# A graph kernel's set-up stage: chunk bases by a product, node rows loaded ahead of the edge sources, scaling one group at a time, and checks and late weights moved into the first pass

## The chip, the cores and the metric

The kernel runs on one core of a Trainium2 chip. The metric is the device time of one execution in microseconds (us), as a median over runs. The engines are TensorE (PE; its weight loads are shown as PEld), VectorE (DVE), ScalarE (ACT), GpSimd (POOL) and SyncE (SP). Each engine works through its own queue of instructions; SP only issues DMA transfers here.

## The reference

There are 12,500 nodes with 256 features and 200,000 edges sorted by their destination. First a graph-convolution layer with a residual, then an attention layer with a residual. Cut to what matters:

```python
def gcn_conv(x, W, b, src, dst, n):          # src, dst with a self-loop per node added
    h = x @ W
    deg = segment_sum(ones, dst, n)
    dinv = where(deg > 0, rsqrt(deg), 0)
    return segment_sum(h[src] * (dinv[src] * dinv[dst])[:, None], dst, n) + b

h = maximum(layernorm(x), 0)
h = relu(gcn_conv(h @ W_pre + b_pre, W1, b1, ...))
h = relu(gcn_conv(h, W2, b2, ...))
x = x + (h @ W_post + b_post)
h = maximum(layernorm(x), 0); xt = (h @ weight).reshape(n, 4, 64)
# alpha: softmax over 4 heads, from xt[src], xt[dst] of the first n edges and attn_l, attn_r
x = x + mix of xt[dst[:n]] by alpha, broadcast to the 4 heads
```

## The kernel before, in words

The fast path has a set-up stage, two convolution passes over all edges, and a short attention stage at the end. If a check fails (`bad_row` above 0) a general path runs afterwards; it does not run on these inputs.

The edges are cut into 112 chunks (`NCH`) of 1792 (`CE`), a chunk into 14 tiles (`J`) of 128. In a pass (`convolve`) GpSimd gathers one tile's 128 source rows with one indirect DMA into `fgot` (L999, 64 buffers), VectorE makes one-hot matrices of a chunk's destinations (`fhot`), and TensorE adds the rows up by products (L1004). When a tile of 128 nodes is complete, the steps of `finish1` (first pass) or `finish2` (second) follow; `e()` is the last of `finish1`.

The set-up stage, which the change is about, makes what the first gather needs: `ftable1`, the 98 tiles of normalised and scaled node rows, in DRAM, and `src_t`, the source numbers turned so that they can index. It goes like this.

- SP loads `dst_r` and `src_r` (111 full rows of 1792 numbers and a last, shorter one), then x in 14 groups of 7 tiles (`load_x`, tile `fxt`, L585). There are 11 buffers (`XB`), so groups 11 to 13 are loaded once groups 0 to 2 have been written to the table.
- GpSimd issues 30 small DMAs that pick every tile's first destination (`a_raw`), and then fills constants: `sel`, `iota_r`, `iota_a`, `slide`, `zeros`.
- VectorE makes `dst_f` and `near_f` of `dst_r`; ScalarE makes `src_f` of `src_r` (L636). TensorE and VectorE multiply W_pre by W1 (`wp`, `wpt`, `wf`, L651 to L664).
- TensorE clears the counts with `zeros` (L671) and turns `near_f`, the destinations and the sources in 4 groups each (`turned`, L680), copied out by VectorE (`near_t`) and ScalarE (`to_t`, `src_t`, L685). Two PSUM buffers called `ft` alternate.
- Degrees are counted in 16 blocks, 4 for each of 4 parts. For a block `count_block` lets VectorE make one-hots (`hot_r`, L699) and TensorE add them up; `stats` makes the layernorm sums of one x group. After a part's last block `place` moves the counts to node order: `tiles_b` (ScalarE, L720), `hot_n` (VectorE, L722), `count` and `fdegs` (TensorE). `norms` makes the scales of a part's node tiles and then scales all its groups in one go (3, 3, 4 and 4 groups of 7 tiles, L773 to L785), each followed by its write to the table. It runs for a part one block after the next part has begun; for the last part at the end.
- Then VectorE runs the checks (L804 to L852), and the weights that are needed later are loaded by ScalarE's queue and worked on by VectorE (L869 to L886). The first gather follows.

The work is emitted under a manual schedule: each engine takes its instructions in the order in which the code gives them. So where a line stands decides what waits behind it.

Of the kernel before, what the change touches and what calls it, by code (L numbers as in the profile page):

```python
# [8 lines left out]
F32 = mybir.dt.float32  # L9
# [8 lines left out]
P = 128  # L18
# [395 lines left out]
def fast_path(  # L414
# [69 lines left out]
    nc.vector.memset(eps, EPS)  # L484

# [7 lines left out]
    row_i = const.tile([P, AC], I32, name="row_i")  # L493
    lane = const.tile([P, 1], F32, name="lane")
    nc.gpsimd.iota(lane, pattern=[[0, 1]], base=0, channel_multiplier=1,
                   allow_small_or_imprecise_dtypes=True)

    def load_w(w, name):
        t = const.tile([P, KC, w.shape[1]], F32, name=name)
        nc.scalar.dma_start(t, w.rearrange("(k p) n -> p k n", p=P))  # L500
        return t
# [5 lines left out]
    with tc.tile_pool(name="fprep", bufs=1) as prep:  # L507
# [34 lines left out]
        src_r = load_edges(src, 0, "fsrc_r")  # L542
# [8 lines left out]


        a_raw = prep.tile([I, NPT, L], I32, name="a_raw")
        nc.gpsimd.memset(a_raw, NOWHERE)
        for k in range(NPT):
            whole = min(E // CE - k * CP, CP)
            d = dst[k * CP * CE:(k * CP + whole // L * L) * CE].rearrange(
                "(q l j e) -> j q l e", l=L, j=J, e=P)
            a = a_raw[:, k, :].rearrange("(j q) l -> j q l", q=Q)
            for q in range(whole // L):  # L560
                nc.gpsimd.dma_start(a[:, q, :], d[:, q, :, 0])
            for l in range(whole % L):
                c = k * CP + whole // L * L + l
                nc.gpsimd.dma_start(
                    a[:, whole // L, l:l + 1],
                    dst[c * CE:(c + 1) * CE].rearrange("(j e) -> j e", e=P)[:, 0:1])
        if last < CE:
            j = -(-last // P)
            e = (NCH - 1) * CE
            a = a_raw[:, NPT - 1, L - 1:L].rearrange("(j q) l -> j q l", q=Q)[:, Q - 1]  # L570
            for n in range(j):
                nc.gpsimd.dma_start(a[n:n + 1], dst[None, e + n * P:e + n * P + 1])
# [19 lines left out]
        for g in range(XB):  # L592
            load_x(g)

# [3 lines left out]
        for r0, base, keep in ((0, 0, [-1, LB - 1]), (R, LB, [1, -LB])):  # L600
# [5 lines left out]
        iota_r = prep.tile([P, R, JB * CP], BF16, name="iota_r")  # L606
        nc.gpsimd.iota(iota_r, pattern=[[1, R], [0, JB * CP]], base=0, channel_multiplier=0,
                       allow_small_or_imprecise_dtypes=True)
# [57 lines left out]
        with tc.tile_pool(name="fpsum", bufs=2, space=PSUM) as psum, \  # L666
# [92 lines left out]
            def norms(k):  # L759
# [11 lines left out]
                for g in range(w0 // G, w1 // G):  # L771
# [14 lines left out]
                    if g + XB < NG:  # L786
                        load_x(g + XB)
# [3 lines left out]
            for s, (k, j0) in enumerate(blocks):  # L791
                count_block(k, j0)
                if s < NG:
                    stats(s)
# [493 lines left out]
```

## Time and profile before

| what | value |
|---|---|
| time of the kernel, median of 3 runs | 4307.19 us (4305.39 to 4313.39) |
| the profiled execution's own time | 4960.23 us |
| span in that profile, first to last instruction | 4958.2 us |
| POOL busy, gathers of L999 | 2984.3 us, 3126 of them, 955 ns each |
| PE busy | 2964.7 us |
| DVE busy | 1148.5 us |
| first gather of the first pass starts | 162.01 us |

Busy times and starts are of the one profiled execution, counted from the start of its span. That execution took 653 us longer than the median run. "Idle before" in a row of the profile names what ended the engine's idle time in front of an instruction; "issue" means that nothing the profile shows was waited for.

### The profile page before, as it was taken

The page shows a single profiled execution, that of the slowest core. Times are in us where ns is not written, and L with a number is a line of the kernel's source. Part 1 is how long each engine was busy: PE and PEld are TensorE (multiplying, and loading weights), DVE is VectorE, ACT ScalarE, POOL GpSimd, SP SyncE. Part 2 cuts the span into 40 slices and gives each one's busy share as a digit, 9 for nine tenths or more (in the row PEclk, how much of TensorE's full clock was granted, in tenths as well). Part 3 has the DMA queues.
Part 4 walks back from the last instruction along what each step waited for, and adds up shares of the span by engine and source line. Part 5 has one row for each costly group of instructions (what it writes and reads, how often), then busy time and mean ns, then how long its engine had stood idle before and what let it go on. Part 6 is the DMA issues. An engine that isn't in the chain of part 4 may idle for free.

```text
span 4958.2 us, 34772 instructions
## 1 busy us (share of the span) xinstructions
PE 2964.7 (60%) x10827; PEld 2202.3 (44%) x10827; DVE 1148.5 (23%) x2468; ACT 383.4 (8%) x1054; POOL 3115.8 (63%) x3297
## 2 busy tenths in 40 slices
PE   5345555564555556465626767666777677677853
PEld 4133444343343334344414555555555555555642
DVE  7211111121111212112202222222222222222227
ACT  3100000000000000000000000000000000000112
POOL 2566666666666666666466666666666666666533
PEclk7567777677777777777757777777777777777766
DMA  5433333333333333333333443444444443444335
GB/s 179 133 93 105 106 106 105 104 108 104 106 105 105 104 105 106 105 106 104 101 93 112 113 112 105 113 108 107 110 109 109 110 108 108 109 110 108 97 97 157
DMA packets 301046, 543.62 MB, mean 110 GB/s; under 512 B 84021, under 2 KB 199476, under 8 KB 300852
## 3 DMA queue, kind: packets, MB, share of 16 engines
q0 software_dynamic: 154480, 414.28, 31.3%
q1 hardware_dynamic: 114926, 111.19, 7.4%
q10 hardware_dynamic: 31446, 15.83, 1.1%
q8 instruction: 88, 1.44, 0.1%
q14 instruction: 106, 0.87, 0.1%
HBM read 488.01 MB, written 52.93 MB: 109 GB/s over the span
## 4 chain that ended last, share of the span: by engine, by line
another core or an unknown queue 36%; PE 32%; issue 19%; DVE 4%; ACT 3%; POOL 1%; DMA 1%; ACTq 0%; DVEq 0%; POOLq 0%; SPq 0%
PE facc L1004 18%; PE fpo L1092 3%; PE fpo L1039 2%; PE fpx L1128 2%; PE fpo L1093 2%; PE fpo L1040 1%; POOL fgot L999 1%; PE fturn L952 1%; ACT h L1113 1%; PE fpt L1014 1%; PE fpz L1080 1%; DVE fhot L939 1%; DVE fx L1097 1%; PE fpz L1082 1%
## 5 line engine op out<-in xcount | busy, mean ns | idle before, releaser
L999 POOL DMA_INDIRECT fgot<-ftable,fsrc_t x3126 | 2984.3, 955 | 1595.4 <-issue 822.5
L1004 PE MATMUL facc<-fgot,fhot 128*128 128x257 f32 (+1 forms) x6252 | 1901.8, 456 | 218.1 <-issue 157.2
L1004 PEld LDWEIGHTS facc<-fgot,fhot 128*128 128x128 f32 x6252 | 1392.8, 233 | 564.6 <-issue 297.0
L952 PE MATMUL fturn<-fident,fsums 128*128 128x128 f32 x448 | 117.3, 355 | 626.9 <-issue 484.8
L939 DVE TENSOR_TENSOR fhot<-iota_p,to_t 128x1792 f32<-128x1792 f32 x224 | 447.6, 2000 | 0.1
L952 PEld LDWEIGHTS fturn<-fident,fsums 128*128 128x128 f32 x448 | 75.9, 184 | 690.4 <-issue 529.0
L946 ACT ACTIVATE fsums<-facc 128x257 f32<-128x257 f32 (+1 forms) x224 | 86.2, 385 | 3586.5 <-remote 2411.7
L1097 DVE SCALAR_TENSOR_TENSOR fx<-fpo,fdinv,fxb 128x256 f32<-128x256 f32 x98 | 47.4, 484 | 1289.1 <-PE fpo L1093 837.2
L1039 PE MATMUL fpo<-wf,fin 128*128 128x256 f32 x392 | 142.4, 499 | 329.1 <-issue 242.9
L1128 PE MATMUL fpx<-fwg,ht 128*128 128x4 f32 (+1 forms) x392 | 99.1, 363 | 391.3 <-ACT ht L1120 359.5
L1033 DVE TENSOR_TENSOR fin<-buf,fpt 128x256 f32<-128x256 f32 x98 | 41.1, 420 | 1205.5 <-remote 916.9
L962 DVE TENSOR_TENSOR buf<-buf,fturn 128x256 f32 x224 | 94.5, 422 | 949.8 <-PE facc L1004 414.4
L1128 PEld LDWEIGHTS fpx<-fwg,ht 128*128 128x128 f32 x392 | 88.6, 300 | 427.4 <-ACT ht L1120 388.7
L1039 PEld LDWEIGHTS fpo<-wf,fin 128*128 128x128 f32 x392 | 93.8, 252 | 362.0 <-issue 330.3
L1092 PE MATMUL fpo<-fwo,fz 128*128 128x256 f32 x392 | 171.8, 584 | 80.7 <-ACT fz L1087 78.8
L1199 POOL DMA_INDIRECT fal<-table_l,fsrc_t x98 | 94.0, 959 | 140.4 <-ACT fxg L1192 84.6
L1080 PE MATMUL fpz<-fin,fwb 128*128 128x128 f32 x784 | 147.5, 317 | 10.3 <-issue 10.3
L1092 PEld LDWEIGHTS fpo<-fwo,fz 128*128 128x128 f32 x392 | 104.7, 291 | 102.2 <-ACT fz L1087 83.4
L1080 PEld LDWEIGHTS fpz<-fin,fwb 128*128 128x128 f32 x784 | 118.3, 215 | 26.6 <-issue 16.3
L1190 PE MATMUL fends<-rows,hot_t 128*128 128x260 f32 x196 | 71.2, 517 | 86.8 <-issue 48.4
L1014 PE MATMUL fpt<-fident,self 128*128 128x128 f32 x392 | 100.6, 343 | 22.4 <-issue 19.6
L1014 PE MATMUL fpt<-fident,h 128*128 128x128 f32 x196 | 42.7, 303 | 108.6 <-ACT h L1113 83.0
(176 smaller groups left out, 1754.9 us busy)
## 6 DMA issues: line engine op xcount, KB each, us to landing
fgot<-ftable,fsrc_t POOLq DMA_INDIRECT x3126
ftable<-fxt SPq DMA_DIRECT2D x14, 910.0 KB
self<-ftable SPq DMA_DIRECT2D x98, 130.0 KB
ftable<-fo ACTq DMA_DIRECT2D x98, 128.0 KB
self<-ftable SPq DMA_DIRECT2D x98, 128.0 KB
kept_x<-fx SPq DMA_DIRECT2D x98, 128.0 KB
fxr<-kept_x SPq DMA_DIRECT2D x14, 896.0 KB
fxb<-in_x_dram SPq DMA_DIRECT2D x97, 128.0 KB
```

The source lines that it names most:

```text
L939: nc.vector.tensor_tensor(h[:, :n, :], iota_p[:, None, :].to_broadcast([P, n, P]), to_t[:, c, :n, None].to_broadcast([P, n, P]), ALU.is_equal)
L952: nc.tensor.transpose(v["pt"][:, k, :], sb[:, k * P:(k + 1) * P], ident)
L962: nc.vector.tensor_add(b, b, v["pt"][:, :KC, :])
L999: nc.gpsimd.indirect_dma_start(out=got, out_offset=None, in_=table[:], in_offset=bass.IndirectOffsetOnAxis(ap=src_t[:, c, j:j + 1], axis=0))
L1004: nc.tensor.matmul(acc, hots[c][:, j, :], got[:, :width], start=(j == 0), stop=(j == nj[c] - 1))
L1014: nc.tensor.transpose(pt[:, k, :], s[:, k * P:(k + 1) * P], ident)
L1039: nc.tensor.matmul(po, v["f"][:, k, :], wf[:, k, :], start=(k == 0), stop=False)
L1080: nc.tensor.matmul(pz[:, m, :], wb[:, k, m * P:(m + 1) * P], v["f"][:, k, :], start=(k == 0), stop=False)
L1092: nc.tensor.matmul(po, v["z"][:, m, :], wo[:, m, :], start=(m == 0), stop=False)
L1093: nc.tensor.matmul(po, v["rm"], bor, start=False, stop=True)
L1097: nc.vector.scalar_tensor_tensor(x2, v["po"], dinv[:, w:w + 1], v["x"], op0=ALU.mult, op1=ALU.add)
L1128: nc.tensor.matmul(px[:, d0:], v["ht"][:, k, :], wg[:, k, d0:], start=(k == 0), stop=(k == KC - 1))
```

## The change

- The chunk tiles' first destinations no longer come by 30 small DMAs. Three VectorE operations and one TensorE product (`low_q`, `by_kl`, `pa`) make them from `low`; the product stands behind all three calls of `turned`. The four operations that make `a_bf` move from the first `place` to the front of the first block.
- `src_r` is loaded after x groups 0 and 1 instead of ahead of x. GpSimd's constants change their order: `zeros`, `slide` and `iota_r` first.
- `dst_f` is gone: `near_f` and `to_f` are made of `dst_r` directly.
- ScalarE instead of VectorE copies `wpt`, `wf`, `bb` and `near_t`. A ScalarE operation on `eps` (`warm`) is put at the very front.
- `stats` runs one block ahead. `norms` only puts its groups in a list; `scale` takes one group per block, and the rest of the list before the last `norms`, with VectorE's help. The copy of `dinv` into the rows moves to GpSimd. One reciprocal for `dinv2` at the end replaces four.
- Part of the checks becomes small GpSimd operations early in the set-up stage; the rest (`check_chunks`) and the loading of the late weights (`load_late`) are emitted in the first pass, behind the first finished node tile.

The diff, cut to its core:

```diff
+    warm = const.tile([P, 1], F32, name="warm")
+    nc.scalar.activation(warm, eps, AF.Sqrt)
...
-        src_r = load_edges(src, 0, "fsrc_r")
...
-        a_raw = prep.tile([I, NPT, L], I32, name="a_raw")
-        nc.gpsimd.memset(a_raw, NOWHERE)
-        for k in range(NPT):
-            whole = min(E // CE - k * CP, CP)
...
-                nc.gpsimd.dma_start(a[:, q, :], d[:, q, :, 0])
...
         for g in range(XB):
             load_x(g)
...
+            if g == 1:
+                src_r = load_edges(src, 0, "fsrc_r")
...
+        zeros = prep.tile([1, 512], BF16, name="zeros")
+        nc.gpsimd.memset(zeros, 0.0)
...
+        perm = prep.tile([NCH, Q, NPT, L], F32, name="perm")
+        nc.gpsimd.memset(perm, 0.0)
+        nc.gpsimd.affine_select(out=perm, in_=perm, compare_op=ALU.not_equal, fill=1.0, base=0,
+                                pattern=[[-L, Q], [-CP, NPT], [-1, L]], channel_multiplier=1)
...
-        dst_f = prep.tile([NCH, CE], F32, name="fdst_f")
-        nc.vector.tensor_copy(dst_f, dst_r)
...
-                                dst_f.rearrange("c (j e) -> c j e", e=P),
+                                dst_r.rearrange("c (j e) -> c j e", e=P),
...
+        by_q = prep.tile([NCH, Q], F32, name="by_q")
+        nc.vector.tensor_reduce(by_q, perm.rearrange("c q k l -> c q (k l)"), AX.X, ALU.add)
+        by_kl = prep.tile([NCH, NPT, L], F32, name="by_kl")
+        nc.vector.tensor_reduce(by_kl, perm.rearrange("c q k l -> c k l q"), AX.X, ALU.add)
+        low_q = prep.tile([NCH, J, Q], F32, name="low_q")
+        nc.vector.tensor_mul(low_q, low[:, :, None].to_broadcast([NCH, J, Q]),
+                             by_q[:, None, :].to_broadcast([NCH, J, Q]))
         base = prep.tile([NCH, 1], F32, name="base")
-        nc.vector.tensor_copy(base, dst_f[:, 0:1])
-        to_f = dst_f
-        nc.vector.tensor_scalar(to_f, dst_f, base, None, op0=ALU.subtract)
+        nc.vector.tensor_copy(base, dst_r[:, 0:1])
+        to_f = prep.tile([NCH, CE], F32, name="fto_f")
+        nc.vector.tensor_scalar(to_f, dst_r, base, None, op0=ALU.subtract)
         src_f = prep.tile([NCH, CE], F32, name="fsrc_f")
         nc.scalar.activation(src_f, src_r, AF.Copy)
...
+        nc.gpsimd.tensor_scalar(mean, mean, 0.0, None, op0=ALU.max)
+        mean_i = prep.tile([NCH, 1], I32, name="mean_i")
+        nc.gpsimd.tensor_copy(mean_i, mean)
+        nc.vector.tensor_scalar(mean_i, mean_i, ~(P - 1), None, op0=ALU.bitwise_and)
...
+        nc.gpsimd.tensor_sub(off, base, off)
...
-                nc.vector.tensor_copy(wpt[:, k, :], pt)
+                nc.scalar.activation(wpt[:, k, :], pt, AF.Copy)
...
-                nc.vector.tensor_copy(wf[:, i, :], pw)
+                nc.scalar.activation(wf[:, i, :], pw, AF.Copy)
...
-            nc.vector.tensor_copy(bb[:1, :], pw[:1, :])
+            nc.scalar.activation(bb[:1, :], pw[:1, :], AF.Copy)
...
-            turned(near, near_t, nc.vector.tensor_copy)
+            turned(near, near_t, by_act)
             turned(to_f, to_t.rearrange("p c j -> p j c"), by_act)
             turned(src_f, src_t.rearrange("p c j -> p j c"), by_act)
-            a_int = prep.tile([I, NPT, L], I32, name="a_int")
             a_bf = prep.tile([I, NPT, L], BF16, name="a_bf")
+            pa = psum.tile([I, NPT, L], F32, name="ft")
+            nc.tensor.matmul(pa, low_q.rearrange("c j q -> c (j q)"), by_kl, start=True, stop=True)
...
-                for g in range(w0 // G, w1 // G):
-                    t = xs[g]
-                    nc.vector.tensor_copy(t[:, :, D], dinv[:, g * G:(g + 1) * G])
-                    for i in range(G):
-                        w = g * G + i
-                        h = t[:, i, :D]
-                        if k == NPT - 1 and i % 2:
-                            nc.vector.tensor_scalar(h, h, sc[:, w:w + 1], nb[:, w:w + 1],
-                                                    op0=ALU.mult, op1=ALU.add)
-                            nc.vector.tensor_scalar(h, h, 0.0, None, op0=ALU.max)
-                        else:
-                            nc.scalar.activation(h, h, AF.Relu, bias=nb[:, w:w + 1],
-                                                 scale=sc[:, w:w + 1])
-                    nc.sync.dma_start(
-                        table1[g * G * P:(g + 1) * G * P, :].rearrange("(c p) d -> p c d", p=P), t)
-                    if g + XB < NG:
-                        load_x(g + XB)
-                nc.vector.reciprocal(dinv2[:, w0:w1], deg[:, w0:w1])
-
+                to_scale.extend(range(w0 // G, w1 // G))
+
+            to_scale = []
+
+            def scale(both):
+
+                g = to_scale.pop(0)
+                t = xs[g]
+                nc.gpsimd.tensor_copy(t[:, :, D], dinv[:, g * G:(g + 1) * G])
+                for i in range(G):
+                    w = g * G + i
+                    h = t[:, i, :D]
+                    if both and i % 2:
+                        nc.vector.tensor_scalar(h, h, sc[:, w:w + 1], nb[:, w:w + 1],
+                                                op0=ALU.mult, op1=ALU.add)
+                        nc.vector.tensor_scalar(h, h, 0.0, None, op0=ALU.max)
+                    else:
+                        nc.scalar.activation(h, h, AF.Relu, bias=nb[:, w:w + 1],
+                                             scale=sc[:, w:w + 1])
+                nc.sync.dma_start(
+                    table1[g * G * P:(g + 1) * G * P, :].rearrange("(c p) d -> p c d", p=P), t)
+                if g + XB < NG:
+                    load_x(g + XB)
+
+            stats(0)
+            for k in range(NPT):
+                nc.vector.tensor_scalar(a_bf[:, k, :], pa[:, k, :], 1.0 / LB, -float(a_of[k]),
+                                        op0=ALU.mult, op1=ALU.add)
             blocks = [(k, j0) for k in range(NPT) for j0 in range(0, J, JB)]
             for s, (k, j0) in enumerate(blocks):
                 count_block(k, j0)
-                if s < NG:
-                    stats(s)
+                if s + 1 < NG:
+                    stats(s + 1)
                 if j0 + JB >= J:
                     place(k)
                 if k and j0 == JB:
                     norms(k - 1)
+                if to_scale:
+                    scale(False)
+            while to_scale:
+                scale(True)
             norms(NPT - 1)
+            while to_scale:
+                scale(True)
+            nc.vector.reciprocal(dinv2, deg)
...
-        nc.vector.tensor_reduce(lo, to_f, AX.X, ALU.min)
...
+        nc.tensor.transpose(pk[:, 0, :NCH], off, ident[:NCH, :NCH])
+        nc.vector.tensor_copy(offs, pk[:, 0, :NCH])
...
+    def check_chunks(work, psum):
+
+        last = E - (NCH - 1) * CE
+        far = work.tile([P, 2, NCH], F32, name="far2", bufs=1)
+        nc.vector.tensor_reduce(far[:, 0, :], to_t, AX.X, ALU.min)
+        c, (n, r) = NCH - 1, divmod(last, P)
...
+    def load_late(work):
+
+        for t, w in ((wb, w2), (wo, w_post), (wg[:, :, :D], w_gat)):
+            nc.scalar.dma_start(t, w.rearrange("(k p) n -> p k n", p=P))
+        nc.scalar.dma_start(b2r, b2[None, :])
+        nc.scalar.dma_start(bor, b_post[None, :])
+
         for i, a in enumerate((attn_r, attn_l)):
-            ar = work.tile([P, D], F32, name="far")
+            ar = work.tile([P, D], F32, name="far", bufs=1)
             nc.scalar.dma_start(ar, a.rearrange("h c -> (h c)").partition_broadcast(P))
...
+            if w == 0:
+                load_late(work)
+                check_chunks(work, psum)
```

## The prediction

> **What bounds the kernel now.** I read the page first: its head and the costliest row.
>
> ```profile
> span 4958.2 us, 34772 instructions
> L999 POOL DMA_INDIRECT fgot<-ftable,fsrc_t x3126 | 2984.3, 955 | 1595.4 <-issue 822.5
> ```
>
> Each gather takes 0.955 us and the next starts 0.30 us later in the timeline, so 3126 of them need at least 3126 × 1.25 = 3908 us. In this profile they come every 1.43 us. The median run, 4307.19 us, is 653 us below the profiled 4960.23, and if I take away the set-up (162), the gap between the passes (44) and the end (280), it has 3821 us or 1.22 us for each gather. So GpSimd's issuing paces both passes, and whatever moves the first gather moves the end, one for one. I take differences from the profile's set-up and put them on the median, which assumes that the set-up stage itself is not stretched by profiling.
>
> Next, the set-up in windows of 2 us (columns: PE, PEld, DVE, ACT, POOL busy; clock; DMA share; GB/s).
>
> ```profile
> 12.00:14.00 2.00, 0.00 (x0) 0.00 (x0) 0.00 (x0) 0.00 (x0) 2.00 (x4) 1.00 0.22 76
> 18.00:20.00 2.00, 0.00 (x0) 0.00 (x0) 1.93 (x4) 0.00 (x0) 2.00 (x4) 1.00 0.21 79
> 34.00:36.00 2.00, 0.32 (x1) 0.12 (x2) 0.00 (x0) 0.00 (x0) 1.66 (x5) 0.50 1.01 331
> ```
>
> For 10 us only 0.21 of the 16 DMA engines, about three, are moving data: the loads of `dst_r` and `src_r`, one after the other. Then the timeline of the front:
>
> ```profile
> 17.37 1.09 DVE L621 CAST fdst_f<-fdst_r 112x1792 f32<-112x1792 int32 x1 [14.94 <-DMA fdst_r<-in_dst_dram]
> 29.28 1.28 ACT L636 ACT_TABLE_LOAD   x1 [29.28 <-DMA fsrc_r<-in_src_dram]
> 35.68 1.03 PE L671 MATMUL count<-zeros 1*32 1x512 bf16 x2 [8.27 <-POOL zeros L617]
> 40.25 2.02 DVE L699 TENSOR_TENSOR hot_r<-near_t,iota_r 128x3584 bf16<-128x3584 bf16 x1
> ```
>
> ScalarE stands still until `src_r` has landed at 29.3; TensorE waits for `zeros`, last in GpSimd's queue. From 40.25 VectorE is busy nearly without a hole until 119.2. The timeline of the stage's end:
>
> ```profile
> 117.47 1.73 DVE L722 TENSOR_TENSOR hot_n<-a_bf,iota_a 56x1526 bf16<-56x1526 bf16 x1
> 128.01 0.33 ACT L720 ACTIVATE tiles_b<-tiles 56x224 bf16<-56x224 f32 x1
> 134.22 0.19 DVE L763 TENSOR_SCALAR fdeg<-fdegs 128x28 f32<-128x28 f32 x1 [15.02 <-PE fdegs L747]
> 143.79 1.96 DVE L804 TENSOR_REDUCE flo<-fdst_f 112x1 f32<-112x1792 f32 x1
> 162.01 1.04 POOL L999 DMA_INDIRECT fgot<-ftable,fsrc_t  x1 [63.64 <-issue]
> ```
>
> `tiles_b` waits 8.8 us behind 28 scalings on ScalarE. From 143.8 the checks and the late weights run. SP's waits say when the table was complete:
>
> ```profile
> SPq L1023 <- DMA ftable<-fxt: 8.8, 1, 8.8
> ```
>
> SP stood at 144.1, so the table landed at 152.9; the gather came 9.1 us later, behind VectorE's work on the weights.
>
> **The change, part by part.** Front first. `src_r` now stands behind x groups 0 and 1 on SP's queue. A group is 0.92 MB; its sixteenth, 57 KB, takes 2.3 us on an engine at 76/3 = 25 GB/s. The Trainium skill, "DMA: Bandwidth & Descriptors", says why this costs the full amount: under "Why a DMA increments its semaphore by 16 and not by 1", a DMA gets the largest number of engines up to 16 that divides the outer size (111 rows: 3), and under "Queues, rings and completion order", descriptors of one ring are consumed in order. The measured 0.21 of 16 agrees. So `src_r` lands at 29.3 + 2 × 2.3 = 33.9. Were it not held up in the ring, it would stay at 29.3; I take the ring. The 30 small DMAs gone may give it up to 1 us back; I count nothing.
>
> ScalarE's queue still has `src_f` at its head, and now `wpt`, `wf`, `bb` and `near_t` are copied by ScalarE behind it, so TensorE waits too. Step by step: `src_f` 1.70 (no table load now, `warm` did it: 1.28 saved) to 35.6; two `wpt` copies at about 0.42 (`fsums`, 385 ns, is the nearest row) to 36.5; the W products took 22.46 to 27.41, 4.95, to 41.5; `bb` 0.4; zeros 1.03, to 43.0. `zeros` itself is no longer waited for, nor GpSimd: its constants are then 14 us of rows that show, starting at 2. Twelve groups are turned: four copied by ScalarE took 40.09 to 44.19, 4.10, so 12.3, to 55.3. Here a rule speaks for less. "ScalarE: Activation LUTs", under "What ACT_TABLE_LOAD costs", gives an immediate-operand ACTIVATE 186 ns + 0.833 ns per column, 559 ns for 448 columns; the trace's median for `to_t` is 948. By the rule the twelve groups would take 12.3 − 6 × 0.39 = 10.0, as every second copy is on the path. The trace decides. Then `pa` (two matmul records of 0.39, overlapping) 0.5 and `a_bf` 0.7: the first `hot_r` starts at 56.5 instead of 40.25. x, loaded early or not, has all landed by then, so its earlier start buys nothing.
>
> Costed at nothing in the front, because VectorE, GpSimd and the first weight loads have nothing to do with the wait for `src_r`: `dst_f` gone (1.09), the three operations that prepare `pa`, and the weight loads' issue behind `warm` (a table load of 1.28; the product of `wp` is wanted at 36 now). If `src_r` came at 20, the first two would be on the path with about a microsecond each way. The 14 or so small GpSimd operations of the moved checks have no near row; between 0.14 (the iota of `fmean`) and 1.08 (a select on `sel`) each, they take 2 to 15 us, begin when `base` is there at 21, and are wanted only at the stage's end. VectorE's one operation among them waits for GpSimd's constants, until 16, with nothing behind it before 56.
>
> The blocks, VectorE: 78.95 us before (40.25 to 119.2). Gone are `stats(0)`, which fits in the wait (2.77), a hole of 1.07, `a_int` and `a_bf` 0.5, ten `dinv` copies 0.73, three reciprocals 0.6: 5.7 less, 73.3. So the last `hot_n` ends at X = 129.8, 10.6 later than the 119.2 before. GpSimd's `dinv` copies (between a 0.13 memset and 0.3) may wait behind a `load_x` memset for a table write (8.7 us in the trace), but x groups 11 to 13 are wanted 20 us later.
>
> The tail, from X. ScalarE has groups 6 and 7 ahead of `tiles_b`: 14 × 0.49 = 6.9 us, begun 4.7 before X, so `tiles_b` starts at X + 2.3 (before: X + 8.8). With count 1.4 and `counted` 0.7 it is X + 5.0; group 8 (3.4) and four of group 9 (2.0) stand ahead of the last `froot`, which comes at X + 10.5 though `fdegs` is ready at X + 8.6 (before: X + 15.2). New wait, small: ScalarE's queue. Then 1.0 for the scales, 8.2 for four groups as before: X + 19.7. Their writes move at about 350 GB/s, 2.65 us each, follow that of group 9 at X + 15.2, and land at X + 26.6; the 0.79 MB of weights no longer share the DMA. VectorE's remaining small checks (some 5 us behind X + 19.7) end before that. Gather at X + 27.0 = 156.8, against 162.0: **5.2 us earlier**. The tail wins 15.8 (6.5 for `tiles_b`, 9 behind the table), the front and blocks give back 10.6.
>
> Moved into the first pass: four products and reductions 4 × 0.836 = 3.3, two reductions of 1568 columns (1.96 for 1792: 1.7 each), a dozen small ones at 0.15 to 0.28: about 9 us of VectorE, and a wait of up to 8 for seven DMAs on ScalarE's queue (issues 0.41 to 1.32 before). Queued behind it are `fhot` of the next chunk and the `buf` additions, so TensorE may stand up to 17 us. GpSimd waits for none: it has 64 buffers, 80 us. Cost 0 if so; at most 2, if a gather here and there takes 1.45 instead of 0.95 as at 999.7; I take 0.5. Without those buffers all 17 would count.
>
> Sum: 4307.2 − 5.2 + 0.5 = **4302.5 us**.
>
> **Rivals.** (A) The front is set back less: `src_r` lands near 29, or copies run by the rule, and the first `hot_r` starts by 53. Each us comes off one for one. Were `src_r` waited for only where it is turned, TensorE would reach `pa` near 40: gain 21, 4286. With 4.6 + 2.3 together: 12, 4295. For it: the 3 engines leave 13 idle. Against: ScalarE's 29.28 us of waiting in front of L636. (B) Slower: `src_r` loses more to x. Each further x group that gets onto its three engines ahead of it adds 2.3 to 2.6; with two the gain is gone, from six on it is slower by over 0.2%, all nine give + 22: 4324. For it: SP's x issues follow at once. Against: ring order. (C) The late work reaches GpSimd: only if VectorE is held for over 75 us; nothing shown is that long.
>
> **How the numbers follow.** 0.2%, 8.6 us, is about what a measurement of this kernel can tell from no change. The likeliest case (0.51) has `hot_r` uncertain by 2.5 and the tail by 3: 4297 to 4308, within 0.2%. A gets 0.42, since three separate steps can each turn out shorter, and B and C 0.07 together. The range reaches into A: 4286 to 4310.
>
> **What would show it.** In the changed profile: ScalarE idle to about 34 in front of `src_f`; first `hot_r` at 54 to 59, behind `a_bf`; x complete before it; last `tiles_b` about 2 us behind `hot_n`; first gather near 157, as the table lands; VectorE waiting in the first pass once, with GpSimd's gathers undisturbed. A first `hot_r` below 50, or a first gather below 152, would make me wrong on the fast side; `src_r` landing past 40 on the slow side.

## The result, and the profile after

| | before | after |
|---|---|---|
| time, median | 4303.65 us (7 runs) | 4292.27 us |
| ratio to before, 95% interval | | 0.9973 [0.9963, 0.9984] |
| first gather of the first pass | 162.17 us | 153.86 us |
| first `hot_r` | 40.55 us | 53.27 us |

The kernel became 11.4 us faster, 7 to 16 by the interval. The forecast was 4302.5, with 4286 to 4310 as its range: the sign is right, and the gain is 2.4 times the 4.7 that had been worked out. The column "before" takes its two starts from a second profile of the same kernel (run before_again, span 4297.7 us). Two slow executions (5724 us of the kernel after, and 4651 us of the kernel before beside a later run) count in no ratio, and on one occasion (runs order and order_split) the kernel before took 5003.56 us, at a mean granted TensorE clock of 0.72 instead of 0.85, so that the times of that occasion stand beside their own kernel before only.

The page after: its head, and the row that paces both passes (busy time, mean ns; idle time in front and what ended most of it).

```profile
span 4287.1 us, 34745 instructions
...
L1012 POOL DMA_INDIRECT fgot<-ftable,fsrc_t x3126 | 2978.4, 953 | 982.9 <-PE facc L1017 449.3
```

The same row of the second profile of before:

```profile
L999 POOL DMA_INDIRECT fgot<-ftable,fsrc_t x3126 | 2978.5, 953 | 1030.0 <-issue 474.1
```

Read the idle time. It includes the stretch just ahead of the first gather, 63.51 us before and 16.39 after. Without it, both kernels leave 966.5 us between gathers. The waits in the passes did not change; the difference lies in when the passes begin.

The timeline after, at the front of the set-up (start, us, engine, line, operation; in brackets the idle time before it and what ended it):

```profile
18.94 0.17 DVE L604 TENSOR_SCALAR low_i<-fdst_r 112x14 int32<-112x14 int32 x1 [16.50 <-DMA fdst_r<-in_dst_dram]
...
35.70 1.70 ACT L625 ACTIVATE fsrc_f<-fsrc_r 112x1792 f32<-112x1792 int32 x1 [33.40 <-DMA fsrc_r<-in_src_dram]
...
42.70 0.99 PE L695 MATMUL ft<-fident,near_f 112*128 112x112 f32 x8
...
45.23 0.98 PE L695 MATMUL ft<-fident,fto_f 112*128 112x112 f32 x8 [0.39 <-ACT near_t L700]
...
48.49 1.75 PE L695 MATMUL ft<-fident,fsrc_f 112*128 112x112 f32 x8 [0.27 <-ACT to_t L700]
...
52.97 0.37 DVE L807 TENSOR_SCALAR a_bf<-ft 56x7 bf16<-56x7 f32 x4 [26.96 <-PE ft L707]
...
53.27 2.00 DVE L715 TENSOR_TENSOR hot_r<-near_t,iota_r 128x3584 bf16<-128x3584 bf16 x1
```

`src_f` is where the prediction looked for it, at the head of ScalarE's queue, and VectorE then waits 27 us for `pa`, the last product behind the turning. The same timeline at the end of the set-up:

```profile
125.98 1.74 DVE L732 TENSOR_TENSOR hot_n<-a_bf,iota_a 56x1526 bf16<-56x1526 bf16 x1
...
128.87 0.33 ACT L730 ACTIVATE tiles_b<-tiles 56x224 bf16<-56x224 f32 x1
...
136.25 0.21 ACT L775 ACTIVATE froot<-fdeg 128x28 f32<-128x28 f32 x1
...
153.31 0.81 DVE L942 MEMSET buf<- 128x896 f32 x1 [4.51 <-DMA ftable<-fxt]
...
153.86 1.24 POOL L1012 DMA_INDIRECT fgot<-ftable,fsrc_t  x1 [16.39 <-issue]
```

`tiles_b` now comes 1.2 us behind the end of the last `hot_n` (127.72). The last table write has landed at 152.7; both VectorE's clear (153.31) and the first gather (153.86) had waited for it. Before, 9 us of checks and weights on VectorE stood between that landing and the gather.

### The profile page after: what moved, and what is told of

The parts are those of the page before. It is cut to its first block, busy times and chain, and to the rows that moved or that the text cites. A ratio compares the mean times of both kernels' runs of the same rounds, so it can differ in the third digit from the quotient of the medians.

```text
span 4287.1 us, 34745 instructions
## 1 busy us (share of the span) xinstructions
PE 3175.4 (74%) x10831; PEld 1912.3 (45%) x10831; DVE 1146.8 (27%) x2439; ACT 384.3 (9%) x1060; POOL 3101.6 (72%) x3295
## 4 chain that ended last, share of the span: by engine, by line
DMA 45%; PE 33%; issue 11%; POOL 8%; DVE 1%; ACT 0%; ACTq 0%; POOLq 0%; DVEq 0%; SPq 0%
DMA fgot<-ftable,fsrc_t 44%; PE facc L1017 21%; POOL fgot L1012 6%; PE fpz L1096 2%; PE fpo L1052 2%; POOL fal L1215 2%; PE fpz L1098 2%; PE fpo L1108 1%; PE fpt L1027 1%; PE fpo L1053 1%; PE fpo L1109 1%; PE fpx L1144 1%; DMA fal<-table_l,fsrc_t 1%; PE fturn L965 0%; ACT fxt L798 0%
## 5 line engine op out<-in xcount | busy, mean ns | idle before, releaser
L1017 PE MATMUL facc<-fgot,fhot 128*128 128x257 f32 (+1 forms) x6252 | 2308.8, 481 | 919.4 <-DMA fgot<-ftable,fsrc_t 877.6
L1017 PEld LDWEIGHTS facc<-fgot,fhot 128*128 128x128 f32 x6252 | 1165.2, 221 | 1896.9 <-DMA fgot<-ftable,fsrc_t 1707.9
L1046 DVE TENSOR_TENSOR fin<-buf,fpt 128x256 f32<-128x256 f32 x98 | 41.2, 421 | 990.8 <-PE fpt L1042 990.8
L1096 PE MATMUL fpz<-fin,fwb 128*128 128x128 f32 x784 | 138.0, 302 | 0.0
L1108 PE MATMUL fpo<-fwo,fz 128*128 128x256 f32 x392 | 120.6, 435 | 1.1 <-DVE fx L1113 0.7
L1096 PEld LDWEIGHTS fpz<-fin,fwb 128*128 128x128 f32 x784 | 111.8, 204 | 13.7 <-issue 1.8
L965 PE MATMUL fturn<-fident,fsums 128*128 128x128 f32 x448 | 101.4, 314 | 0.2 <-ACT fsums L959 0.2
L1098 PE MATMUL fpz<-rm,fb2r 1*128 1x128 f32 x392 | 99.8, 336 | 0.0
L1206 PE MATMUL fends<-rows,hot_t 128*128 128x260 f32 x196 | 61.9, 484 | 45.6 <-ACT fxg L1208 45.4
L988 DVE COPY buf<-buf 128x640 f32<-128x640 f32 x196 | 87.2, 445 | 0.0
L1090 DVE TENSOR_TENSOR fin<-buf,fpt 128x256 f32<-128x256 f32 x98 | 38.6, 394 | 160.8 <-PE fpt L1027 160.8
L1108 PEld LDWEIGHTS fpo<-fwo,fz 128*128 128x128 f32 x392 | 76.5, 212 | 11.0 <-issue 1.6
```

What stands on the lines that cost most here:

```text
L965: nc.tensor.transpose(v["pt"][:, k, :], sb[:, k * P:(k + 1) * P], ident)
L988: nc.vector.tensor_copy(nxt[:, :, :BW - P], buf[:, :, P:])
L1017: nc.tensor.matmul(acc, hots[c][:, j, :], got[:, :width], start=(j == 0), stop=(j == nj[c] - 1))
L1096: nc.tensor.matmul(pz[:, m, :], wb[:, k, m * P:(m + 1) * P], v["f"][:, k, :], start=(k == 0), stop=False)
L1098: nc.tensor.matmul(pz[:, m, :], b2r[:, m * P:(m + 1) * P], v["rm"], start=False, stop=True)
L1108: nc.tensor.matmul(po, v["z"][:, m, :], wo[:, m, :], start=(m == 0), stop=False)
```

## Experiments

The table sets the start of the first gather in each run's profile against that of before_again (162.17), and the run's median time against that of the kernel before, measured on the same chip and occasion. "Pass 1" is the first to the last gather of the first pass, from the timeline.

| run | first gather | against 162.17 | time against before | ratio [95%] | pass 1 |
|---|---|---|---|---|---|
| before_again | 162.17 | 0 | +0.7 | 1.0001 [0.9992, 1.0009] | 1965.8 |
| late_back | 171.97 | +9.8 | +9.5 | 1.002 [1.0011, 1.0029] | 1967.4 |
| one_go | 160.10 | −2.1 | −4.4 | 0.9991 [0.9984, 0.9998] | 1968.6 |
| (after) | 153.86 | −8.3 | −11.4 | 0.9973 [0.9963, 0.9984] | 1968.3 |
| late_x4 | 154.34 | −7.8 | −10.6 | 0.9977 [0.9967, 0.9987] | 1968.1 |
| src_first | 147.83 | −14.3 | −15.2 | 0.9965 [0.9952, 0.9979] | 1967.7 |
| pa_early | 147.95 | −14.2 | −19.8 | 0.9957 [0.9943, 0.997] | 1968.4 |
| srcf_late | 142.59 | −19.6 | −19.8 | 0.9953 [0.994, 0.9967] | 1967.0 |
| split_rows | 138.04 | −24.1 | −26.8 | 0.9935 [0.9922, 0.9949] | 1967.5 |
| order_again | 131.28 | −30.9 | −32.5 | 0.9924 [0.9911, 0.9938] | 1964.1 |
| order_split_again | 124.80 | −37.4 | −37.6 | 0.9913 [0.99, 0.9927] | 1963.8 |

Over a span of 47 us in the start of the gathers, the time follows it within 6 us at worst and usually 3, while pass 1 stays within 5 us. That carries the prediction's first claim, that whatever moves the first gather moves the end, one for one.

**Was the set-up stretched in the first profile?** The kernel before, unchanged:

> The kernel before, unchanged, for a second profile. The first profile of it ran 653 us above the median run, with its passes stretched. If only the passes were stretched and the set-up stage was not (the assumption of the prediction), the first gather starts at 162 us again, give or take 1, and the span falls to about 4300. If the set-up had been stretched too, the first gather would start well before 162, and the difference of 8.1 us to the changed kernel's 153.9 would be smaller than it looked.

The second profile, of an execution 660 us shorter, has the first gather here:

```profile
162.17 1.03 POOL L999 DMA_INDIRECT fgot<-ftable,fsrc_t  x1 [63.51 <-issue]
```

The first had 162.01. Of the extra 660 us, 565 were idle time between the gathers (1595.4 against 1030.0), 90 lay behind the last gather, and none ahead of the first. So the starts that the prediction read from the stretched profile were good; what it read there of the gap between the passes and of the end was not.

**The order of the loads.** `src_r` goes back behind `dst_r`, ahead of x:

```diff
+        src_r = load_edges(src, 0, "fsrc_r")
...
-            if g == 1:
-                src_r = load_edges(src, 0, "fsrc_r")
```

> The changed kernel with one part undone: src_r is loaded directly behind dst_r, ahead of all x, as before. Theory (the late landing of src_r holds ScalarE and with it the whole front): src_f starts near 29.5 instead of 35.7, first hot_r near 47 instead of 53.3, first gather near 147.7 instead of 153.9, time 6 us below the changed kernel. Rival (x needed that early: the blocks then wait for x): first hot_r earlier, but VectorE waits for x inside the blocks, and the gather gains less than 3 us.

`src_f` started at 29.07 instead of 35.70, and the gather came 6.0 us earlier. So the change's new place for `src_r` costs some 6 us; it is a part of the change that works against it. Nor did x come sooner for it: the last of the first 11 groups was complete at 57.7 us in the kernel after, and at 56.3 in src_first.

Where the 6 us arise can be read in the transfers of the kernel after. A row of an index load is a packet of 7 KB, a row of x one of 1 KB. First the stretch from 4 to 17.8 us, then 17.8 to 22.9, then 22.9 to 35:

```profile
DMA packets 1894, 2.31 MB, mean 168 GB/s; under 512 B 306, under 2 KB 1782, under 8 KB 1894
DMA packets 795, 0.81 MB, mean 159 GB/s; under 512 B 5, under 2 KB 795, under 8 KB 795
DMA packets 1187, 1.87 MB, mean 154 GB/s; under 512 B 33, under 2 KB 1075, under 8 KB 1187
```

There are 112 packets over 2 KB in the first stretch, the rows of `dst_r`, and 112 in the last, those of `src_r`. In the 5.1 us between them only x moves. In src_first the rows of `dst_r` end at 14.5 us, 3.3 sooner, and those of `src_r` follow at 14.7. SP's waits in the kernel after (in total, times, longest):

```profile
SPq L561 <- DMA ftable<-fxt: 17.3, 3, 7.7
SPq L535 <- DMA fdst_r<-in_dst_dram: 7.2, 1, 7.2
```

The second row: SP had two groups of x issued at 11.6 us, and then stood 7.2 us, until `dst_r` had landed, before it issued `src_r` at 18.87. In the run src_first the x groups meet the same wait, 12.1 us. By these times the late issue did not hold `src_r`'s data: its rows moved 4.1 us behind the issue, where those of `dst_r` had moved 2.3 us behind theirs. What makes SP wait for the earlier load was not separated.

**`src_f` out of the way.** ScalarE makes `src_f` only where it is turned:

```diff
-        nc.scalar.activation(src_f, src_r, AF.Copy)
...
             turned(to_f, to_t.rearrange("p c j -> p j c"), by_act)
+            nc.scalar.activation(src_f, src_r, AF.Copy)
             turned(src_f, src_t.rearrange("p c j -> p j c"), by_act)
```

> The changed kernel with the conversion src_f moved on ScalarE's queue from the front to directly ahead of the turning of the sources. Theory (it is the order on ScalarE's queue, not src_r itself, that holds the W product and the first two sets of turnings): W product by 10, near turned from about 21.5, destinations turned by 28, src_f still at 35.7, pa at 42, first hot_r near 43 instead of 53.3, first gather near 143.5, 10 us below the changed kernel. Rival (pa needs src_r in any case, so the order is worth only what lies between src_f and the sources' turning once more in parallel): less than 4 us.

```profile
21.99 1.23 ACT L699 ACTIVATE near_t<-ft 128x448 bf16<-128x448 f32 x2 [7.29 <-PE ft L694]
...
27.30 1.31 ACT L699 ACTIVATE to_t<-ft 128x448 f32<-128x448 f32 x2 [0.32 <-PE ft L694]
...
35.14 1.70 ACT L703 ACTIVATE fsrc_f<-fsrc_r 112x1792 f32<-112x1792 int32 x1 [6.53 <-DMA fsrc_r<-in_src_dram]
...
41.38 0.37 DVE L807 TENSOR_SCALAR a_bf<-ft 56x7 bf16<-56x7 f32 x4 [15.98 <-PE ft L707]
```

In this timeline the destinations are turned by 28.6, in the time in which `src_r` is still under way; `src_f` itself starts only half a microsecond earlier (35.14), yet `a_bf` is 11.6 us earlier, and so is the gather (11.3). ScalarE's queue held `near_t` and `to_t` back, not the data.

**The product for the tiles' first ends, earlier.** It needs nothing of the sources:

```diff
             turned(near, near_t, by_act)
+            pa = psum.tile([I, NPT, L], F32, name="ft")
+            nc.tensor.matmul(pa, low_q.rearrange("c j q -> c (j q)"), by_kl, start=True, stop=True)
             turned(to_f, to_t.rearrange("p c j -> p j c"), by_act)
             turned(src_f, src_t.rearrange("p c j -> p j c"), by_act)
```

> The changed kernel with the product pa and nothing else moved, directly behind the turning of near. Theory (the first block waits for pa, and pa stands behind two sets of turnings that it does not need): first hot_r near 46 instead of 53.3, first gather 7 us earlier, near 147, time 7 us below the changed kernel; destinations and sources are turned beside the first block. Rival (TensorE's first counts then wait behind the two sets, so the gain is lost in the blocks): less than 3 us.

`src_f` stays at 35.76, the first `hot_r` comes at 47.21 instead of 53.27, and the gather at 147.95. (The time fell by 5.6 us more than the start tells; its interval, 13 to 25 us, holds the 14.) So 6 us of the front are the turning of `to_f` and `src_f`, ahead of a product that does not use it.

**The rows of the index loads.** A load of 111 rows is issued as 96 and 15:

```diff
-            nc.sync.dma_start(t[:NCH - 1, :],
-                              e[:(NCH - 1) * CE].rearrange("(c e) -> c e", e=CE))
+            for c0, c1 in ((0, 96), (96, NCH - 1)):
+                nc.sync.dma_start(t[c0:c1, :],
+                                  e[c0 * CE:c1 * CE].rearrange("(c e) -> c e", e=CE))
```

> The changed kernel with one edit: each of the two loads of 111 rows is cut into 96 and 15 rows. Theory (111 rows go to 3 of the 16 engines, 96 to 16 and 15 to 15, and src_r's landing holds the front): dst_r lands near 9 instead of 18.9, src_r near 15 instead of 35.6, first hot_r near 33 instead of 53.3, first gather near 134, time 20 us below the changed kernel. Rival (the loads are bound by something else, such as row size or the issuing queue): no change in the landings.

The set-up in windows of 2 us; the column before the last is the share of the 16 DMA engines. First the kernel after:

```profile
18.00:20.00 2.00, 0.00 (x0) 0.00 (x0) 0.99 (x3) 0.00 (x0) 0.00 (x0) 1.00 0.20 66
26.00:28.00 2.00, 0.00 (x0) 0.00 (x0) 0.01 (x1) 0.00 (x0) 0.03 (x1) 1.00 0.20 82
```

Then this run:

```profile
8.00:10.00 2.00, 0.00 (x0) 0.00 (x0) 0.48 (x1) 0.00 (x0) 1.93 (x3) 1.00 1.07 294
12.00:14.00 2.00, 0.00 (x0) 0.00 (x0) 2.00 (x3) 0.00 (x0) 2.00 (x1) 1.00 1.15 345
```

and where the two loads were first used in it:

```profile
9.52 1.10 DVE L605 TENSOR_SCALAR low_i<-fdst_r 112x14 int32<-112x14 int32 x1 [7.08 <-DMA fdst_r<-in_dst_dram]
...
18.94 1.70 ACT L626 ACTIVATE fsrc_f<-fsrc_r 112x1792 f32<-112x1792 int32 x1 [16.64 <-DVE fstats L765]
```

`dst_r` is used at 9.52 instead of 18.94, `src_r` at 18.94 instead of 35.70 (the row names VectorE, but the last rows of `src_r` had moved only by 17.95), and the gather is 15.8 us earlier. The windows of this run have x in them too, so the share alone is no proof; the rows of `dst_r` moved from 3.75 to 7.2 us, where they had taken from 4.05 to 17.8. The gain stayed below the 20 us expected, with `src_r` 4 us later than expected. Nothing else was changed: no other single edit here was worth as much as taking both index loads off about three of the 16 engines.

**Scaling in one go.** `norms` scales all its groups at once again:

```diff
                 to_scale.extend(range(w0 // G, w1 // G))
+                while to_scale:
+                    scale(k == NPT - 1)
```

> The changed kernel with the scaling undone: norms again scales all groups of its part in one go. Theory (group by group saves only what stood ahead of the last tiles_b, and gives part of it back as a wait of froot behind groups 8 and 9): tiles_b of the last part starts near 135.8 instead of 128.9, the last froot near 141 instead of 136.3, the first gather near 158 instead of 153.9, time 4 us above the changed kernel. Rival (scaling group by group is what the whole gain comes from): time 10 us above, back at the kernel before.

```profile
122.66 13.87 ACT L800 ACTIVATE fxt<-fxt,fnb,fsc 128x256 f32<-128x256 f32 x28 [0.89 <-DVE fnb L779]
...
136.44 0.33 ACT L730 ACTIVATE tiles_b<-tiles 56x224 bf16<-56x224 f32 x1
...
142.88 0.23 ACT L775 ACTIVATE froot<-fdeg 128x28 f32<-128x28 f32 x1 [3.92 <-DVE fdeg L773]
```

and the kernel after:

```profile
121.97 6.99 ACT L798 ACTIVATE fxt<-fxt,fnb,fsc 128x256 f32<-128x256 f32 x14 [0.89 <-DVE fnb L779]
```

Here 28 scalings in a row stand ahead of `tiles_b`, in the kernel after 14. `tiles_b` comes 7.6 us later, `froot` 6.6, the gather 6.2. So scaling group by group is worth 6 us. The prediction had given 6.5 to `tiles_b`, counted from X, the end of the last `hot_n`. Counted so it is 5.3, since X itself comes 2.3 us later here (130.02), mostly because VectorE waits longer for TensorE's `tiles`.

**The late work.** `load_late` and `check_chunks`, in their new form, go back ahead of the first pass:

```diff
+    with tc.tile_pool(name="fwork", bufs=2) as work, \
+            tc.tile_pool(name="lpsum", bufs=1, space=PSUM) as psum:
+        load_late(work)
+        check_chunks(work, psum)
...
-            if w == 0:
-                load_late(work)
-                check_chunks(work, psum)
```

> The changed kernel with the late weights and the remaining checks put back in front of the first pass. Theory (they cost about what lay behind the landed table before, 9 us, and nothing inside the pass): VectorE does 3.4 us of weights and 6.5 us of checks from about 149 on, first gather near 161 instead of 153.9, time 7 us above the changed kernel. Rival (the 14.6 us that VectorE was held at 229 to 248 of the first pass cost gathers too): then putting the work back gives some of that back, and the time rises by less than 4 us.

The gather came 18.1 us later than in the kernel after. The expectation had summed VectorE's work and left out two waits. In the timeline:

```profile
154.71 0.36 ACTq L895 DMA_DIRECT2D far<-in_L_gnn_attn_r_dram  x1
159.74 0.36 ACTq L895 DMA_DIRECT2D far<-in_L_gnn_attn_l_dram  x1
...
158.37 0.43 DVE L898 TENSOR_TENSOR fprod<-fwg,far 128x256 f32<-128x256 f32 x1 [9.93 <-DMA fins<-root_t]
...
162.79 0.42 DVE L898 TENSOR_TENSOR fprod<-fwg,far 128x256 f32<-128x256 f32 x1 [2.63 <-DMA far<-in_L_gnn_attn_l_dram]
...
171.97 1.24 POOL L1017 DMA_INDIRECT fgot<-ftable,fsrc_t  x1 [34.84 <-issue]
```

The first `far` is issued only at 154.71, as the set-up ends, and is there 3.7 us later. (The row of `fprod` puts that wait down to another transfer, `fins`; the issue right ahead of it is that of `far`.) The second is issued only when VectorE has used the first (159.74), because `far` has one buffer now. VectorE's work then runs from 158.37 to 170.9, on the path. In the other direction, the late work was done four times over where the change has put it:

```diff
             if w == 0:
-                load_late(work)
-                check_chunks(work, psum)
+                for _ in range(4):
+                    load_late(work)
+                    check_chunks(work, psum)
```

> The changed kernel with the late loads and the checks in the first pass done four times in a row: the same results, VectorE held about 4 times 19 us. Theory (GpSimd runs 64 gathers ahead, 80 us, so one such hold costs nothing and four reach the end of the buffers): the time rises by 0 to 15 us, all of it as GpSimd waiting for TensorE once near 310. If VectorE's hold cost gathers from the first us on, the rise would be some 60 us. If TensorE or VectorE paced the pass, it would be 60 too.

The windows of this run (PE, PEld, DVE, ACT and POOL busy, clock, DMA share, GB/s):

```profile
240.00:260.00 20.00, 1.68 (x4) 0.58 (x4) 12.38 (x27) 0.00 (x0) 15.19 (x16) 0.50 0.72 208
260.00:280.00 20.00, 2.10 (x6) 0.66 (x5) 13.32 (x37) 0.00 (x0) 15.30 (x16) 0.50 0.64 165
...
300.00:320.00 20.00, 20.00 (x99) 16.32 (x98) 8.77 (x21) 1.50 (x4) 15.12 (x17) 1.00 0.52 138
```

VectorE's `fhot` of the next chunk comes at 291.02, 70 us after VectorE's last work for the pass. TensorE all but stops in the first two windows and works it off from 291 on, at full busy and full clock. GpSimd's column stays at 15.1 to 15.3 in each. Pass 1 is as long as in the kernel after, so the 64 buffers of `fgot`, 80 us of gathers, bridge a hold of 70 us; a longer one was not tried.

**A better order.** `src_r` behind all of x; the turnings of `to_f` and `src_f` one group at a time between the blocks of the counts; `pa` directly behind `near`; for order_split the 96 and 15 rows besides:

```diff
-            turned(to_f, to_t.rearrange("p c j -> p j c"), by_act)
-            turned(src_f, src_t.rearrange("p c j -> p j c"), by_act)
...
             for s, (k, j0) in enumerate(blocks):
...
+                j = s % 4 * 4
+                if s < 4:
+                    turned(to_f, to_t.rearrange("p c j -> p j c"), by_act, [j])
+                if 8 <= s < 12:
+                    if s == 8:
+                        nc.scalar.activation(src_f, src_r, AF.Copy)
+                    turned(src_f, src_t.rearrange("p c j -> p j c"), by_act, [j])
```

> src_r is loaded behind all of x, src_f is made and the turnings of to_f and src_f are made between the blocks of the sort (s = 0 to 3 and s = 8 to 11), so that ahead of the first hot_r only dst's near part and the product for pa stand. If the path of the front is dst alone (theory): the first hot_r starts at 25 to 28 us instead of 53.27, provided that the product for pa needs nothing of src; the blocks may be stretched by the inserted turnings by up to 4 us, the first gather starts near 126 to 132 (153.86 in the kernel after), and the time is 22 to 28 us below the kernel after, 4264 to 4271 us. Rival: src_r, now behind x, lands so late that the turning of src_f holds ScalarE, and with it the blocks or the last tiles, so that no more than the 11 us of making src_f late remains: 4279 to 4284 us.

> The same as the run order, with the first 111 rows of both index loads issued as 96 and 15 rows. dst_r landed 9.4 us earlier so in the run split_rows. If dst's landing still leads the front (theory): first hot_r 9 us earlier than in the run order, first gather near 117 to 123, 4255 to 4262 us. Rival: once the front is this short, something else ends it (the constants that GpSimd makes, or the loads of x and of the weights), and the split adds less than 4 us to the run order.

On that occasion the ratios to before were 0.9949 [0.9934, 0.9965] and 0.9939 [0.9915, 0.9963]: 24 and 27 us less by the medians, with the first gather at 130.81 and 125.92. The gathers' idle time was 1595 us instead of 984, so both stand here a second time.

> The kernel of the run order_split once more, since that run and its kernel before were both some 16% longer than usual, with a granted clock of 0.72 instead of 0.85, and GpSimd waited in the passes. Its set-up already had the first gather at 125.92, against 153.86 in the kernel after and 162.17 in the kernel before. If the set-up counts one to one where GpSimd's cadence of 1.25 us sets the passes (theory): 36 us below the kernel before, 4266 us, give or take 4. Rival: less than 25 us of it arrive, because GpSimd then waits in the passes for something that the set-up no longer covers, 4277 us or more; the row of the gathers would then show more than 985 us of idle time.

> The kernel of the run order once more, for the same reason. Its first gather stood at 130.81 there. Theory: 31 us below the kernel before, 4271 us, give or take 4, so that the row split is worth 5 us on top of the new order, against some 15 us by itself in the run split_rows. Rival: 4277 us or more, with GpSimd's waits in the passes grown.

4261.5 and 4266.55 us, against 4299.09 of before: 37.6 and 32.5 less. order_split is the fastest kernel of the study. The turnings between the blocks are not free: from the first `hot_r` to the end of the last `hot_n` it takes 80.1 us in order_again, against 74.4 in the kernel after. The row split is worth 6.5 us of the start on top of the new order, not the 15.8 it had alone. There `src_r` was on the path; here its rows have moved by 56 us and `src_f` is made at 71.8, so only `dst_r` is left on it. Of the 9.9 us by which it is used sooner, the first `hot_r` gains 5.4 (20.41 against 25.84; 9 had been expected). What holds the front next, in order_split_again:

```profile
8.73 0.71 DVE L604 TENSOR_SCALAR low_i<-fdst_r 112x14 int32<-112x14 int32 x1 [6.30 <-DMA fdst_r<-in_dst_dram]
...
15.56 0.39 PE L704 MATMUL ft<-by_kl,low_q 112*56 112x28 f32 x2 [0.26 <-ACT near_t L699]
...
17.31 0.15 DVE L641 TENSOR_SCALAR mean_i<-mean_i 112x1 int32<-112x1 int32 x1 [1.78 <-POOL mean_i L640]
...
17.38 2.37 DVE L761 BATCH_NORM_STATS2 fstats<-fxt 128x6 f32<-128x256 f32 x7
...
20.15 0.33 DVE L804 TENSOR_SCALAR a_bf<-ft 56x7 bf16<-56x7 f32 x4
```

`pa` is ready at 15.95. `a_bf` follows only at 20.15, behind a check that waits for GpSimd and behind `stats(0)`, both ahead of it in VectorE's queue. Moving these two was not tried.

## Why the prediction was right, and where its sizes were off

The sign, the mechanism and the place of each part were right. The likeliest case, 4297 to 4308, did not come: the time lies in the stretch that the prediction gave to rival A. The working went wrong in the sizes of a few terms of its sum:

| step | predicted | trace after |
|---|---|---|
| `src_r` landed, `src_f` starts | 33.9 | 35.70 |
| turning starts | 43.0 | 42.70 |
| twelve turned groups | 12.3 | 9.9 |
| first `hot_r` | 56.5 | 53.27 |
| end of the last `hot_n` (X) | 129.8 | 127.72 |
| `tiles_b` | X + 2.3 | X + 1.2 |
| last `froot` | X + 10.5 | X + 8.5 |
| table landed | X + 26.6 | X + 25.0 |
| first gather | X + 27.0 = 156.8 | X + 26.1 = 153.86 |
| late work in the pass | 0.5 (0 to 2) | 0 |

**The bound.** The sum by which the prediction came to 3821 us for the gathers does not hold: that is less than its own floor of 3908. It had taken the gap between the passes (44) and the end (280) from the long execution. In before_again they are 16 and 191, and the passes take 1965.8 and 1962.4 us, 1.26 for each gather. The conclusion, that GpSimd's issuing paces both passes, stands.

**The front.** "So `src_r` lands at 29.3 + 2 × 2.3 = 33.9" fell 1.8 short. The wait behind the two groups of x was right, at 5.1 us for the 4.6 worked out. What the step took as unchanged was the load ahead of them: the rows of `dst_r` end at 17.8 us, where they had ended at 16.3 before. The way from `src_f` to the turning was 7.0 us instead of 9.1, a bit less at each link: 2.0 to the first W product (2.6 predicted), 4.5 for the products with those of the bias (4.95), nothing for `bb` (0.4), 0.6 for `zeros` (1.03).

**Twelve groups at 4.10 for four.** This is the largest miss, 2.4 us. By kind: `near` took 2.5 us (42.70 to 45.23), `to_f` 3.3 and `src_f` 4.1. Only the last takes what the row used by the prediction took. There are two differences. First, a `near_t` copy took 540 ns in the middle, not the 933 of `to_t`, from the same 448 columns of PSUM. The Trainium skill's figure ("ScalarE: Activation LUTs", under "What ACT_TABLE_LOAD costs") that the prediction set aside, 559 ns, fits `near_t` and does not fit `to_t`. `near_t` is bf16 and written in order, `to_t` float and written across; which of the two makes the difference was not separated. Second, TensorE's granted clock was full for `near` and most of `to_f` and half for `src_f`, where it had been half for all twelve groups before. Two windows of the kernel after (columns as above):

```profile
46.00:48.00 2.00, 1.18 (x9) 0.63 (x7) 0.00 (x0) 2.00 (x3) 0.00 (x0) 0.94 1.04 322
48.00:50.00 2.00, 1.73 (x10) 1.41 (x8) 0.00 (x0) 1.29 (x3) 0.00 (x0) 0.50 1.04 340
```

and one of before, as the turning begins:

```profile
36.00:38.00 2.00, 2.00 (x9) 1.36 (x8) 0.31 (x1) 0.00 (x0) 0.00 (x0) 0.50 0.99 321
```

Eight products took 0.98 and 0.99 us for `near` and `to_f`, and 1.75 for `src_f`. So the total that the prediction worked out by the rule and set aside, 10.0, came out nearly exact by luck: the rule fits four of the twelve groups, and the clock did the rest.

**The blocks and the tail.** From the first `hot_r` to X it took 74.4 us, predicted 73.3; before it was 79.0. A hole of 1.15 us in which VectorE waited for TensorE's `tiles` at 123 had not been foreseen. In the tail each step came 1 to 2 us sooner than predicted. The scalings were those of the prediction, 14 ahead of `tiles_b` and 11 ahead of `froot`. But the 14 began 5.7 us ahead of X, not 4.7, and `count` took 0.81 us at a granted clock of 1.00, where the row of before, 1.38, was taken at 0.50. The tail won 16.5 us, predicted 15.8. "x has all landed by then" was wrong too: x was complete at 57.7 us, 4.4 behind the first `hot_r`. No wait for x in the blocks came of it.

**Sum.** Of the 8.3 us that the trace gained, 5.2 had been predicted. The other 3 are the front's 3.2 and the tail's 0.9, less the blocks' 1.1. The times gained 11.4, with an interval that holds 8.3.

**The rivals.** A, the front set back less, is what happened in part: `hot_r` at 53.27 against its mark of 53, though not because `src_r` came sooner. Its stronger form, `src_r` waited for only where it is turned, had been given 21 us against before; srcf_late measured 19.8. B, more groups of x on the three engines ahead of `src_r`, did not happen: the wait was 5.1 us, that of two groups. The new place still cost the 6 us that src_first shows, which the change could have kept. C, the late work reaching GpSimd, needed a hold of over 75 us. The change's hold was 28 us, where 17 had been the estimate, and even four times the work left GpSimd alone:

```profile
235.75 0.42 DVE L898 TENSOR_TENSOR fprod<-fwg,far 128x256 f32<-128x256 f32 x1 [15.10 <-DMA far<-in_L_gnn_attn_r_dram]
...
248.38 2.00 DVE L952 TENSOR_TENSOR fhot<-iota_p,to_t 128x1792 f32<-128x1792 f32 x1
```

Of the 28 us, 15.1 are the wait for the first `far`; up to 8 had been estimated for all the waits. Moving the late work had been valued at 9 us, by what stood on the path before. In its new form it would have cost 18 there.

## What to carry to other kernels

Where one engine paces a long pass, find what its first instruction waits for, follow that back through each queue, and ask of each step whether it needs what stands ahead of it in the queue: here `pa`, `near_t` and `to_t` needed nothing of `src_r`. Taking them out of its shadow, with `src_r` behind all of x (order_again), brought the gathers 22.6 us forward, on top of the 8.3 of the whole change. Look at the DMA share in a wait for data: a load at 0.20 of the engines can be cut into pieces whose row counts use them all. When an operation has no row in the profile, a row of the same size but another output type or layout, or from a stage at another granted clock, can be off by nearly a half.

## What the runs showed of the hardware

- Cutting 111 rows into 96 and 15 let `dst_r` be used at 9.52 us instead of 18.94; its rows moved in 3.5 us instead of 13.7. The rule of the page "DMA: Bandwidth & Descriptors" of the Trainium skill (section "Why a DMA increments its semaphore by 16 and not by 1"), which the prediction used for the three engines, gives all 16 for 96 rows; the runs agree.
- Behind `dst_r` and two groups of x, the rows of `src_r` moved only 5.1 us after the last of `dst_r`. SP itself stood 7.2 us in front of the issue of `src_r`, until the load of `dst_r`, issued 17 us before, had landed. So a transfer's place in the queue can delay both its issue and its data.
- TensorE began at the lower speed after standing idle. In the kernel after, the first seven of the products below took 624 to 796 ns each, the eighth, at 40.87 us, 413, and the four behind it 378. The granted clock then fell to 0.50 at 47.7 us, and changed between 0.50 and 1.00 through the rest of the set-up. In front of 40.9 us the windows print 1.00, which the times of these products contradict.

```profile
37.72 3.56 PE L672 MATMUL fw<-fwa,wpt 128*128 128x256 f32 x8 [32.68 <-ACT wpt L668]
41.21 1.02 PE L677 MATMUL fw<-fwa,fbp 128*1 128x256 f32 x4
```

- At a mean granted clock of 0.72 instead of 0.85 (4976 against 4262 us for order_split) the gathers kept their time, 956 against 952 ns each. The idle time between them grew from 984 to 1595 us, and what lies behind the last one by 90. Whether the clock is the cause was not separated.
